# Gathers held twelve pairs back, a zone of 54 pairs, wider one-hots for lots, and waits by tile in one pool

## The chip, the cores and the metric

The kernel runs on one core of a Trainium2 chip. The metric is the device time of one execution in microseconds; a run's time is given beside the span that the profiler saw between the first and the last instruction.

## The reference

Three layers of a graph network with relations, on 6250 nodes of 256 features and 100000 edges, each with one of three types and 32 attributes; the edges come sorted by their target, and the targets crowd at low numbers (a squared uniform draw). Cut to what matters:

```python
ew = edge_attr @ edge_w + edge_b
rel_masks = [(edge_type == i).astype(x.dtype) for i in range(3)]
inv_cnt = [1.0 / jnp.maximum(segment_sum(m, dst, n), 1.0) for m in rel_masks]
x0 = x
for l in range(3):
    residual = x
    msg = relu(x[src] * ew)
    out = zeros((n, 256))
    for i in range(3):
        h = segment_sum(msg * rel_masks[i][:, None], dst, n) * inv_cnt[i][:, None]
        out = out + h @ weights[l, i]
    out = out + x @ roots[l] + biases[l]
    x = residual + relu(out)
return layernorm(x0 + x)
```

## The kernel before, in words

**Tiles and steps.** The edges are cut into tiles of 128, two tiles make a pair (391 pairs), two pairs a quad. For a quad the kernel fetches the source rows with indirect DMAs (one for each tile, so two a pair; `gather_pair`, L1458, issued by POOL into the ring of tiles `xs`, which has room for 8 quads), multiplies them with the edge weights (`weigh`, L873 on DVE), takes the relu (L874 on ACT), builds one-hots of the targets (`one_hot`), and sums the rows by target and relation with matmuls of rows and one-hots (`reduce`). A span is a run of pairs whose sums share a place in PSUM. Where the one-hot is the stationary operand (L911, L914) the sums come out turned: ACT copies them (`take`, L930), PE turns them back (`turn`, L934 and L936). `add` (L962, for lots L944) adds the sums to `acc`, which holds three relations of a window of nodes. When a block of 128 nodes is complete, matmuls with the layer's weights and root make its new rows (L975 to L1025).

**Zone and lots.** The first Z pairs are the zone: the low targets, where many edges share few nodes. Layers 1 and 2 don't go through them pair by pair. In layer 0 each zone quad's weights are kept (`keep_ew`, L800) and scattered row by row into a table in DRAM (`scatter`, L757 on POOL), in an order that a sort on DVE makes in groups of three tiles (L598 to L615). A class is one block of 128 source nodes with one relation (147 classes), and has room for 128 rows. In layers 1 and 2 the zone's edges come from that table by lots: a lot is a quad of up to four classes of one relation, a tile for each (39 lots a layer, 36 of them with four tiles). As a lot's tile has its sources in one block of x_all, PE picks their rows out of it (L836), and lots need no gather. Z came from `zone_of`, which takes the largest even number of pairs whose targets stay within 3 x 40 = 120 nodes: 52. The one-hot has 120 columns: WIN = 40 nodes by three relations for a common pair, 120 nodes of one relation for a lot.

**Order.** One loop over steps `it` (a step is a pair; 391 in layer 0, 391 - 52 + 75 = 414 in layers 1 and 2, of which 75 are lots' pairs) issues for each step, by hand: the sums of the pair of this step, the gathers of the pair AHEAD = 10 steps on, take, turn and add of spans that are done, weights and weighing and one-hots of the pair two steps on, and what a finished node block needs. In layer 0 the zone's quads are put in among the others, 7.1 steps apart, from step K + 114 on (K = 76), and the pairs from Z to 57 come as one block at K + 12. In layer 0, `keep_ew` also stores the weights of each quad beyond the zone to DRAM (L806 on ACT, L807 on SP), and `one_hot` its one-hots (L893, L895); layers 1 and 2 load both (L821 and L886 take them from the loaded tiles). So L890 makes one-hots from the targets in layer 0 and for lots alone.

**The wait of a gather.** `hold` adds to a gather a dependency on the sums of an earlier gathered pair: LEAD = 10 gathered pairs back (for the first 20 gathered pairs LEAD + HEAD = 12 back). `hold_early` does the same for the next layer's first 8 pairs. On POOL's queue a held gather holds what stands behind it: the next gathers and, in layer 0, the scatters that `after` puts behind each.

```python
        def hold(got, u, i):
            g = nth[u]
            if g >= LEAD + HEAD:
                behind(got, fetched[g - (LEAD if g >= 2 * LEAD else LEAD + HEAD)], i)
```

**Memory.** The pool `big` (L486) holds x_all, acc and inv. What lay at its place before is a pool of small tiles used at the start for looking at the indices (seg_o is made from its tiles by L1628). Without `reuse_waits="tile"` every tile of a pool waits until all readers of what the pool's place held are done; with it a tile waits for those alone whose memory it takes.

Of the kernel before, what the change touches and what calls it, by code (L numbers as in the profile page):

```python
# [442 lines left out]
def ordered_path(ctx, tc, x, attr_laid, A, weights, roots, biases, edge_w, edge_b, out, src, src_i, seg, place_i, consts, x_root,  # L443
# [41 lines left out]

    big = ctx.enter_context(tc.tile_pool(name="big", bufs=1))  # L486
    only = ExitStack()
# [205 lines left out]
    def layer(l, r_sb, b_sb, ats, early, ready, pools):  # L693
# [188 lines left out]
        def one_hot(q):  # L882
            ohs[q] = edge.tile([P, 4, WK], F32, name="oh", bufs=3)
            n = tiles_of(q)
            if q in oh_ls:
                nc.scalar.activation(ohs[q][:, :n], oh_ls[q][:, :n], AF.Copy)  # L886
                return
            for i in reversed(range(n)):
                at = zone[q][:, i // 2, i % 2, D:D + 1] if q in zone else seg[:, 4 * q + i:4 * q + i + 1]
                nc.vector.tensor_scalar(ohs[q][:, i, :], iota_w[:, :, :WIN], at, None, op0=ALU.is_equal)  # L890
            if l == 0:
                oh_bs[q] = early_pool.tile([P, 4, WK], BF, name="oh_b", bufs=3)
                nc.scalar.activation(oh_bs[q][:, :n], ohs[q][:, :n], AF.Copy)  # L893
                if 2 * q >= Z:
                    nc.sync.dma_start(oh_all[q][:, :n * WK], oh_bs[q][:, :n].rearrange("p t w -> p (t w)"))  # L895

        def reduce(u):
            span = span_of[u]
            bank, part = banks[span]
            first = opens(u) and part == 0  # L900
# [6 lines left out]
            if turned(span, last):  # L907
                for i in range(n):
                    t = u % 2 * 2 + i
                    if l == 0 and u // 2 in wide:  # L910
                        summed[u, i] = nc.tensor.matmul(h_p[:WK, :D + 1], ohs[u // 2][:, t, :], wide[u // 2][:, u % 2, i, :],  # L911
                                         start=(i == 0 and first), stop=(i == n - 1 and closes(u)), skip_group_check=True)
                        continue
                    summed[u, i] = nc.tensor.matmul(h_p[:WK, :D], ohs[u // 2][:, t, :], rows_of(u, i),  # L914
                                     start=(i == 0 and first), stop=(i == n - 1 and closes(u)), skip_group_check=True)
                    if l == 0:
                        summed[u, i] = nc.tensor.matmul(h_p[:WK, D:D + 1], oh_bs[u // 2][:, t, :], full_ones[:, 0:1],
                                         start=False, stop=(i == n - 1 and closes(u)), skip_group_check=True)
                return
            for i in range(n):  # L920
                for d in range(CH):
                    summed[u, i] = nc.tensor.matmul(h_p[:, d * WK:(d + 1) * WK],  # L922
                                     rows_of(u, i)[:, d * P:(d + 1) * P] if d < DC else full_ones,
                                     (ohs if d < DC else oh_bs)[u // 2][:, u % 2 * 2 + i, :],
                                     start=(i == 0 and d == 0 and first), stop=(i == n - 1 and closes(u)), skip_group_check=True)

        def take(span):
            n = D + 1 if l == 0 else D
            h_ss[span] = edge.tile([P, D + 1], F32, name="h_s", bufs=4)
            nc.scalar.activation(h_ss[span][:WK, :n], h_ps[span][:WK, :n], AF.Copy)  # L930

        def turn(span):
            for d in range(DC):
                nc.tensor.transpose(h_ps[span][:, d * WK:(d + 1) * WK], h_ss[span][:WK, d * P:(d + 1) * P], ident[:WK, :WK])  # L934
            if l == 0:
                nc.tensor.matmul(h_ps[span][:, DC * WK:(DC + 1) * WK], h_ss[span][:WK, D:D + 1].to_broadcast([WK, P]),  # L936
                                 ident[:WK, :WK], start=True, stop=True)

        def add(span):
            u = span[0]  # L940
            if u >= ZU:
                r = lots[u // 2 - ZU // 2][0]
                there = acc[:, :DC, r, ASIDE:ASIDE + WK]
                nc.vector.tensor_tensor(there, h_ps[span][:, :DC * WK].rearrange("p (c w) -> p c w", c=DC), there, op=ALU.add)  # L944
                return
# [271 lines left out]
EARLY = 8  # L1217
LEAD = 10
HEAD = 2
# [27 lines left out]
def zone_of(N, E):  # L1247
# [4 lines left out]
    v = 2  # L1252
    while v < U and node(2 * P * (v + 2)) * (1 + 6 / (2 * P * (v + 2)) ** 0.5) + 2 <= 3 * WIN:
        v += 2
# [213 lines left out]
def kernel(ctx, tc, x, src, dst, edge_attr, edge_type, weights, roots, biases, edge_w,  # L1468
# [11 lines left out]
    U = T // 2  # L1480
    WK = 3 * WIN
    K = schedule(N, E, 1, 0)[0][0]
# [7 lines left out]
    for name, width, value, kind in (("zero_o", 1, 0.0, F32), ("eps", 1, EPS, F32), ("full_ones", P, 1.0, BF)):  # L1490
        filled.append(keep.tile([P, width], kind, name=name))
        nc.vector.memset(filled[-1], value)
    iota_w = keep.tile([P, WK // WIN, WIN + GAP], F32, name="iota_w")
    nc.gpsimd.iota(iota_w, pattern=[[WIN, WK // WIN], [1, WIN + GAP]], base=0, channel_multiplier=0,
                   allow_small_or_imprecise_dtypes=True)
# [13 lines left out]
    with tc.tile_pool(name="look", bufs=1) as look, tc.tile_pool(name="look_p", bufs=2, space=PSUM) as look_p, \  # L1509
# [81 lines left out]
        tail = look.tile([P, 1], F32, name="tail")  # L1591
        for u, v, nodes in ((0, Z, WK), (Z, K, 2 * P)):
            nc.vector.tensor_reduce(tail, dst_t[:, 2 * u:2 * v], AX.X, ALU.max)
# [93 lines left out]
```

## Time and profile before

| | us |
|---|---|
| median of three runs | 3497.67 |
| lowest and highest run | 3482.07, 3502.85 |
| the profiled execution | 3495.29 |
| span of the profiled execution | 3493.3 |
| layer 0 / 1 / 2, stretches of the span | 1336 / 1062 / 1067 |
| PE, POOL busy | 2595.5 (74%), 2137.0 (61%) |
| DVE, ACT busy | 1897.1 (54%), 1891.7 (54%) |

In a profile "busy" is time in which an engine executes an instruction; PE is TensorE's matmuls and PEld its weight loads, DVE is VectorE, ACT ScalarE, POOL GpSimd, SP SyncE. "Idle before" an instruction is put down to what ended it last: `<-PE h_p L922` is an instruction of that line on that engine, "issue" is time for which the profile shows no wait, and "remote" a semaphore from an unknown source. An indirect DMA's busy time on POOL is the making of its descriptors, not the transfer.

### The profile page before, as it was taken

What the parts mean: (1) busy time and instruction counts of PE and PEld (TensorE: products, weight loads), DVE (VectorE), ACT (ScalarE), POOL (GpSimd) and SP (SyncE); (2) the same over time, 40 slices, a digit from 0 to 9 for tenths busy, and PEclk for the clock granted to TensorE, in tenths of its full rate; (3) what the DMA queues carried; (4) which work ended last, traced back from release to release, by engine and by line L of the source; (5) the groups of instructions that cost most, each with busy time, mean ns of one, the idle gap of its engine ahead of it and who ended that gap; (6) DMA issues with size and microseconds to landing.
All of it is one profiled execution on the core that took longest, in us unless ns stands there. A gap on an engine that the chain in (4) does not pass through costs nothing. (4 is left out here: it accounts for less than half of the span.)

```text
span 3493.3 us, 45265 instructions
## 1 busy us (share of the span) xinstructions
PE 2595.5 (74%) x12880; PEld 1999.6 (57%) x12880; DVE 1897.1 (54%) x4221; ACT 1891.7 (54%) x2580; POOL 2137.0 (61%) x2254
## 2 busy tenths in 40 slices
PE   5778777777777687777777777776777877778766
PEld 2445455555555455555566667665566666667665
DVE  6656555656555464444445555543445555566655
ACT  5666655555555555555554455554555655555555
POOL 6666666666666665666655566665666655565664
PEclk9889888888889899898988898888898999898888
DMA  7888555555555566767666676665776767766764
GB/s 247 274 261 257 189 179 182 177 174 174 173 172 173 165 194 220 229 215 223 211 202 205 203 224 216 216 212 160 257 235 219 230 220 223 227 215 222 225 216 153
DMA packets 358718, 730.97 MB, mean 209 GB/s; under 512 B 59082, under 2 KB 215804, under 8 KB 358332
## 3 DMA queue, kind: packets, MB, share of 16 engines
q1 hardware_dynamic: 243840, 426.68, 36.1%
q0 software_dynamic: 107616, 294.11, 28.4%
q10 hardware_dynamic: 7004, 7.19, 0.7%
q8 instruction: 107, 1.75, 0.2%
q14 instruction: 151, 1.24, 0.1%
HBM read 570.29 MB, written 157.46 MB: 208 GB/s over the span
## 5 line engine op out<-in xcount | busy, mean ns | idle before, releaser
L1458 POOL DMA_INDIRECT xs<-x_mid,src_r x1324 | 1255.9, 949 | 819.8 <-issue 396.8
L1458 POOL DMA_INDIRECT xs<-in_x_dram,src_io x770 | 734.3, 954 | 455.5 <-issue 161.8
L874 ACT ACTIVATE xs<-xs 128x1024 f32<-128x1024 f32 x533 | 560.4, 1051 | 767.1 <-DVE xs L873 484.5
L922 PE MATMUL h_p<-oh,xs 128*128 128x120 f32 x4608 | 716.1, 306 | 227.9 <-DVE acc L962 79.8
L922 PEld LDWEIGHTS h_p<-oh,xs 128*128 128x128 f32 x4608 | 671.7, 216 | 300.8 <-issue 115.7
L873 DVE TENSOR_TENSOR xs<-ew_p,xs 128x1024 f32<-128x1024 f32 x533 | 643.6, 1211 | 109.3 <-issue 48.9
L962 DVE TENSOR_TENSOR acc<-h_p,acc 128x240 f32 (+1 forms) x761 | 339.9, 449 | 662.7 <-remote 201.5
L991 PE MATMUL o_p<-w_sb,acc 128*128 128x256 f32 (+1 forms) x1752 | 505.3, 431 | 108.9 <-DVE acc L962 35.3
L991 PEld LDWEIGHTS o_p<-w_sb,acc 128*128 128x128 f32 (+1 forms) x1752 | 360.4, 216 | 209.9 <-issue 64.6
L914 PE MATMUL h_p<-xs,oh 128*120 128x256 f32 x1176 | 324.6, 409 | 80.9 <-ACT oh L886 24.9
L1022 DVE SCALAR_TENSOR_TENSOR x_root<-o_p,inv,x_root 128x256 f32<-128x256 f32 (+1 forms) x438 | 211.1, 482 | 303.4 <-PE o_p L991 93.3
L821 ACT ACTIVATE ew_p<-ew_s 128x1024 f32<-128x1024 f32 (+1 forms) x340 | 343.7, 1011 | 5.9 <-DMA ew_s<-ew_all 5.0
L914 PEld LDWEIGHTS h_p<-xs,oh 128*120 128x120 f32 x1176 | 222.6, 198 | 135.5 <-issue 50.4
L806 ACT ACTIVATE keep<-ew_p 128x1024 f32<-128x1024 f32 x170 | 172.4, 1014 | 202.0 <-remote 80.6
L850 PE MATMUL ew_p<-x_root,at 64*128 64x512 f32 x606 | 199.6, 738 | 79.1 <-issue 39.0
L911 PE MATMUL h_p<-xs,oh 128*120 128x257 f32 x772 | 213.4, 406 | 59.9 <-issue 36.6
L874 ACT ACTIVATE zone<-zone 128x1024 f32<-128x1024 f32 (+1 forms) x78 | 78.7, 1009 | 323.5 <-issue 156.6
L914 PE MATMUL h_p<-zone,oh 128*120 128x256 f32 x576 | 178.0, 447 | 99.8 <-ACT zone L874 36.8
L1008 ACT ACTIVATE acc<-zero_o 128x768 f32<-128x768 f32 (+1 forms) x150 | 141.4, 943 | 139.3 <-PE o_p L991 48.7
L836 PE MATMUL ew_p<-x_all,hot 128*128 128x256 f32 x588 | 164.5, 428 | 66.7 <-DVE hot L829 34.3
L890 DVE TENSOR_SCALAR oh<-iota_w,seg_o 128x120 f32<-128x120 f32 x782 | 207.8, 328 | 0.0
L911 PEld LDWEIGHTS h_p<-xs,oh 128*120 128x120 f32 x772 | 138.0, 191 | 109.3 <-issue 59.8
(182 smaller groups left out, 2870.3 us busy)
## 6 DMA issues: line engine op xcount, KB each, us to landing
ew_s<-ew_all SPq DMA_DIRECT2D x338, 512.0 KB
ew_all<-keep SPq DMA_DIRECT2D x169, 512.0 KB
oh_l<-oh_all SPq DMA_DIRECT2D x338, 120.0 KB
zone<-zone_table SPq DMA_DIRECT2D x72, 516.0 KB
xs<-x_mid,src_r POOLq DMA_INDIRECT x1324
oh_all<-oh_b SPq DMA_DIRECT2D x169, 120.0 KB
zone_table<-blank SPq DMA_DIRECT2D x21, 677.2 KB
x_mid<-x_all SPq DMA_DIRECT2D x98, 128.0 KB
```

What stands on the lines that cost most here:

```text
L821: nc.scalar.activation(ew_ps[q][:, :n], ew_ss[q][:, :n], AF.Copy)
L850: nc.tensor.matmul(ew_ps[q][:, k].rearrange("p i d -> p (i d)"), at[half, :], ew_sb[half].rearrange("p i d -> p (i d)"), start=False, stop ...
L873: nc.vector.tensor_mul(there, ew_ps[q][:, pairs.start:pairs.stop, :n], there)
L874: nc.scalar.activation(there, there, AF.Relu)
L890: nc.vector.tensor_scalar(ohs[q][:, i, :], iota_w[:, :, :WIN], at, None, op0=ALU.is_equal)
L911: summed[u, i] = nc.tensor.matmul(h_p[:WK, :D + 1], ohs[u // 2][:, t, :], wide[u // 2][:, u % 2, i, :], start=(i == 0 and first), stop=(i ...
L914: summed[u, i] = nc.tensor.matmul(h_p[:WK, :D], ohs[u // 2][:, t, :], rows_of(u, i), start=(i == 0 and first), stop=(i == n - 1 and closes ...
L922: summed[u, i] = nc.tensor.matmul(h_p[:, d * WK:(d + 1) * WK], rows_of(u, i)[:, d * P:(d + 1) * P] if d < DC else full_ones, (ohs if d < D ...
L962: nc.vector.tensor_tensor(there, h_ps[span][:, :CH * WK].rearrange("p (c r w) -> p c r w", c=CH, r=R), there, op=ALU.add)
L991: nc.tensor.matmul(o_p[:n, j, :], acc[:, d, r, slot:slot + n], w_sb[:, r * DC + d, :], start=(d == 0), stop=(d == DC - 1))
L1022: nc.vector.scalar_tensor_tensor(root, o_p[:n, j, :], inv[:n, c, r:r + 1], root, op0=ALU.mult, op1=ALU.add)
L1458: got = nc.gpsimd.indirect_dma_start(out=xs[:, u % 2, i, :], out_offset=None, in_=x_rows[:, :], in_offset=bass.IndirectOffsetOnAxis(ap=src ...
```

## The change

- `LEAD` goes from 10 to 12: a gather waits for the sums of the pair gathered twelve before it (the first 24 gathered pairs: fourteen before it). The steps at which gathers are issued stay.
- `zone_of` allows 128 nodes for 120: Z goes from 52 to 54. Layers 1 and 2 have 412 steps for 414, with as many lots, whose rows are fuller; pairs 52 and 53 are gathered in layer 0 alone, as a 27th quad of the zone (at step 374), whose weights go to the table, and no longer in the block at K + 12.
- A lot's one-hots, sums, takes, turns and adds are 128 columns wide (`wide_of`). The tile `oh` has room for 4 x 128; other pairs use 120 columns of each 128. L890 writes 128 columns in four pieces of 32 from an `iota_w` of four pieces, 40 apart, where it wrote 120 in one run from three pieces of 40, 48 apart.
- `big` gets `reuse_waits="tile"`.
- The look at the indices that decides whether this path can be used allows 128 nodes in the zone.

```diff
-    big = ctx.enter_context(tc.tile_pool(name="big", bufs=1))
+    big = ctx.enter_context(tc.tile_pool(name="big", bufs=1, reuse_waits="tile"))
...
         def one_hot(q):
-            ohs[q] = edge.tile([P, 4, WK], F32, name="oh", bufs=3)
+            hots_of = edge.tile([P, 4, P], F32, name="oh", bufs=3)
             n = tiles_of(q)
+            ohs[q] = hots_of if q in zone else hots_of[:, :, :WK]
...
-                nc.vector.tensor_scalar(ohs[q][:, i, :], iota_w[:, :, :WIN], at, None, op0=ALU.is_equal)
+                nc.vector.tensor_scalar(hots_of[:, i, :].rearrange("p (a b) -> p a b", a=4), iota_w[:, :, :P // 4], at, None,
+                                        op0=ALU.is_equal)
...
+        def wide_of(span):
+            return P if span[0] >= ZU else WK
+
...
-                    summed[u, i] = nc.tensor.matmul(h_p[:WK, :D], ohs[u // 2][:, t, :], rows_of(u, i),
+                    summed[u, i] = nc.tensor.matmul(h_p[:w, :D], ohs[u // 2][:, t, :], rows_of(u, i),
...
-                there = acc[:, :DC, r, ASIDE:ASIDE + WK]
-                nc.vector.tensor_tensor(there, h_ps[span][:, :DC * WK].rearrange("p (c w) -> p c w", c=DC), there, op=ALU.add)
+                there = acc[:, :DC, r, ASIDE:ASIDE + P]
+                nc.vector.tensor_tensor(there, h_ps[span][:, :DC * P].rearrange("p (c w) -> p c w", c=DC), there, op=ALU.add)
...
-LEAD = 10
+LEAD = 12
...
-    while v < U and node(2 * P * (v + 2)) * (1 + 6 / (2 * P * (v + 2)) ** 0.5) + 2 <= 3 * WIN:
+    while v < U and node(2 * P * (v + 2)) * (1 + 6 / (2 * P * (v + 2)) ** 0.5) + 2 <= P:
...
-    iota_w = keep.tile([P, WK // WIN, WIN + GAP], F32, name="iota_w")
-    nc.gpsimd.iota(iota_w, pattern=[[WIN, WK // WIN], [1, WIN + GAP]], base=0, channel_multiplier=0,
+    iota_w = keep.tile([P, 4, P // 4 + GAP], F32, name="iota_w")
+    nc.gpsimd.iota(iota_w, pattern=[[P // 4, 4], [1, P // 4 + GAP]], base=0, channel_multiplier=0,
...
-        for u, v, nodes in ((0, Z, WK), (Z, K, 2 * P)):
+        for u, v, nodes in ((0, Z, P), (Z, K, 2 * P)):
```

## Rows read from the trace of the kernel before

**Rows 1.** The page's span, and its part 1: busy us, share, instructions of each engine.

```profile
span 3493.3 us, 45265 instructions
PE 2595.5 (74%) x12880; PEld 1999.6 (57%) x12880; DVE 1897.1 (54%) x4221; ACT 1891.7 (54%) x2580; POOL 2137.0 (61%) x2254
```

**Rows 2.** By layer: stretch, us, PE/PEld/DVE/ACT/POOL busy (count), clock, DMA share, GB/s.

```profile
28.00:1364.00 1336.00, 1011.07 (x4896) 678.05 (x4897) 779.71 (x2007) 776.15 (x977) 842.91 (x884) 0.87 0.62 200
1364.00:2426.00 1062.00, 783.70 (x3978) 659.27 (x3976) 517.32 (x946) 536.66 (x750) 639.42 (x675) 0.87 0.68 213
2426.00:3493.00 1067.00, 792.74 (x3995) 660.35 (x3993) 579.25 (x1193) 573.83 (x852) 636.17 (x670) 0.88 0.68 217
```

**Rows 3.** The waits, whole span: engine, tile, line, what ended the wait; us, times, longest.

```profile
POOL xs L1458 <- issue: 564.1, 1485, 5.9
POOL xs L1458 <- PE h_p L922: 167.9, 157, 4.5
```

**Rows 4.** Groups by line, page's part 5: count, busy us, mean ns, idle before, releaser.

```profile
L1458 POOL DMA_INDIRECT xs<-x_mid,src_r x1324 | 1255.9, 949 | 819.8 <-issue 396.8
L1458 POOL DMA_INDIRECT xs<-in_x_dram,src_io x770 | 734.3, 954 | 455.5 <-issue 161.8
```

**Rows 5.** The view of line L873 on DVE: its idle time until a transfer (us, times).

```profile
  DMA xs<-in_x_dram,src_io: 5.7, 5
```

**Rows 6.** Timeline of the start: start, us, engine, line, operation, count, idle before.

```profile
21.62 1.28 ACT L498 ACT_TABLE_LOAD   x1 [21.62 <-DVE seg_o L1628]
22.92 2.12 ACT L498 ACTIVATE acc<-zero_o 128x2304 f32<-128x2304 f32 x1
25.98 1.23 DVE L873 TENSOR_TENSOR x_root<-ew_p,x_root 128x1024 f32<-128x1024 f32 x1 [4.12 <-ACT keep L806]
```

**Rows 7.** Groups by line, whole span.

```profile
L890 DVE TENSOR_SCALAR oh<-iota_w,seg_o 128x120 f32<-128x120 f32 x782 | 207.8, 328 | 0.0
L890 DVE TENSOR_SCALAR oh<-iota_w,zone 128x120 f32<-128x120 f32 x294 | 78.5, 328 | 0.0
L600 DVE TENSOR_SCALAR sort_hot<-iota_c,class_f 128x147 bf16<-128x147 bf16 x104 | 28.7, 276 | 0.0
L615 DVE TENSOR_REDUCE rank<-sort_hot 128x3 bf16<-128x441 bf16 (+1 forms) x35 | 21.4, 611 | 1.2
L821 ACT ACTIVATE ew_p<-ew_s 128x1024 f32<-128x1024 f32 (+1 forms) x340 | 343.7, 1011 | 5.9 <-DMA ew_s<-ew_all 5.0 <-issue 0.9
```

**Rows 8.** The view of line L671: ns min/median/max, first and last start.

```profile
L671 DVE TENSOR_SCALAR came<-came,next_i x16: 274/278/375, 922.3 to 1031.0; 128x128 f32<-128x128 int32 x16
```

**Rows 9.** Timeline of DVE around one-hots in layer 0, a first and a last lot.

```profile
27.13 1.06 DVE L890 TENSOR_SCALAR oh<-iota_w,seg_o 128x120 f32<-128x120 f32 x4
32.48 0.26 DVE L580 TENSOR_SCALAR before<-iota_c,node_i 128x128 bf16<-128x128 bf16 x1 [2.45 <-POOL iota_c L572]
...
1355.88 2.04 DVE L890 TENSOR_SCALAR oh<-iota_w,seg_o 128x120 f32<-128x120 f32 x8
1362.16 0.53 DVE L962 TENSOR_TENSOR acc<-h_p,acc 128x360 f32 x1 [4.24 <-issue]
...
1408.49 1.06 DVE L890 TENSOR_SCALAR oh<-iota_w,zone 128x120 f32<-128x120 f32 x4
1409.47 2.37 DVE L873 TENSOR_TENSOR xs<-ew_p,xs 128x1024 f32<-128x1024 f32 x2
...
3329.83 0.33 DVE L890 TENSOR_SCALAR oh<-iota_w,zone 128x120 f32<-128x120 f32 x1
3330.08 0.40 DVE L962 TENSOR_TENSOR acc<-h_p,acc 128x240 f32 x1
```

**Rows 10.** Timeline of DVE and of POOL about 69 us.

```profile
69.22 1.35 DVE L1002 TENSOR_TENSOR acc<-acc 128x1152 f32<-128x1152 f32 x1
69.30 2.08 POOL L1458 DMA_INDIRECT xs<-in_x_dram,src_io  x1 [0.30 <-issue]
```

More of the change, by code (lines that the diff above doesn't have):

```diff
@@ L895, in one_hot @@
                     nc.sync.dma_start(oh_all[q][:, :n * WK], oh_bs[q][:, :n].rearrange("p t w -> p (t w)"))
+        def wide_of(span):
+            return P if span[0] >= ZU else WK
         def reduce(u):
             span = span_of[u]
+            w = wide_of(span)
             bank, part = banks[span]
@@ L910, in reduce @@
                     if l == 0 and u // 2 in wide:
-                        summed[u, i] = nc.tensor.matmul(h_p[:WK, :D + 1], ohs[u // 2][:, t, :], wide[u // 2][:, u % 2, i, :],
+                        summed[u, i] = nc.tensor.matmul(h_p[:w, :D + 1], ohs[u // 2][:, t, :], wide[u // 2][:, u % 2, i, :],
                                          start=(i == 0 and first), stop=(i == n - 1 and closes(u)), skip_group_check=True)
                         continue
-                    summed[u, i] = nc.tensor.matmul(h_p[:WK, :D], ohs[u // 2][:, t, :], rows_of(u, i),
+                    summed[u, i] = nc.tensor.matmul(h_p[:w, :D], ohs[u // 2][:, t, :], rows_of(u, i),
                                      start=(i == 0 and first), stop=(i == n - 1 and closes(u)), skip_group_check=True)
                     if l == 0:
-                        summed[u, i] = nc.tensor.matmul(h_p[:WK, D:D + 1], oh_bs[u // 2][:, t, :], full_ones[:, 0:1],
+                        summed[u, i] = nc.tensor.matmul(h_p[:w, D:D + 1], oh_bs[u // 2][:, t, :], full_ones[:, 0:1],
                                          start=False, stop=(i == n - 1 and closes(u)), skip_group_check=True)
@@ L921, in reduce @@
                 for d in range(CH):
-                    summed[u, i] = nc.tensor.matmul(h_p[:, d * WK:(d + 1) * WK],
+                    summed[u, i] = nc.tensor.matmul(h_p[:, d * w:(d + 1) * w],
                                      rows_of(u, i)[:, d * P:(d + 1) * P] if d < DC else full_ones,
@@ L928, in take @@
             n = D + 1 if l == 0 else D
+            w = wide_of(span)
             h_ss[span] = edge.tile([P, D + 1], F32, name="h_s", bufs=4)
-            nc.scalar.activation(h_ss[span][:WK, :n], h_ps[span][:WK, :n], AF.Copy)
+            nc.scalar.activation(h_ss[span][:w, :n], h_ps[span][:w, :n], AF.Copy)
         def turn(span):
+            w = wide_of(span)
             for d in range(DC):
-                nc.tensor.transpose(h_ps[span][:, d * WK:(d + 1) * WK], h_ss[span][:WK, d * P:(d + 1) * P], ident[:WK, :WK])
+                nc.tensor.transpose(h_ps[span][:, d * w:(d + 1) * w], h_ss[span][:w, d * P:(d + 1) * P], ident[:w, :w])
             if l == 0:
@@ L1480 @@
     U = T // 2
-    WK = 3 * WIN
+    assert 3 * WIN <= P
     K = schedule(N, E, 1, 0)[0][0]
```

## The prediction, made before the changed kernel was run

> **What bounds the kernel now.** I read the page's head first: no engine fills the span. PE is busy for 2595.5 of 3493.3 us, POOL for 2137.0, DVE and ACT for 54% each [rows 1]. So the kernel is a loop of steps that the engines hand to each other, and what counts is the length of a step. The view by stretches gives it: layer 0 takes 1336 us for 391 steps, 3.42 us each; layer 1 takes 1062 us and layer 2 takes 1067 us for 414 steps, 2.565 and 2.577 us each [rows 2]. In layer 0, PE is busy for 1011 us (76%), DVE for 780 us (58%).
>
> Then the waits, since the change is named after the gathers. POOL stands before L1458 for long: 564.1 us are put down to issue, and 167.9 to the sums of L922 alone [rows 3]. By the groups it is 819.8 + 455.5 = 1275 us before 1324 + 770 = 2094 gathers [rows 4]. Of this the fixed issue time of 0.30 us that stands before a gather even when nothing holds it ("0.30 <-issue" [rows 10]) is 2094 x 0.30 = 628 us; the other 647 us is POOL being held back. The reader is to ask whether anyone behind POOL lacks those 647 us. The consumer of a gather is L873 on DVE. Its line shows idle time until a transfer into xs of 5.7 us, five times, in the whole span [rows 5]. So gathers are held because they are early: they wait for room, and the weighing hardly ever waits for them.
>
> **The change part by part.**
>
> *Gathers two pairs further ahead.* No instruction is added. Each gather's semaphore wait goes from the sums ten gathered pairs back to those twelve back, so POOL runs some two steps (5 to 7 us) earlier. Behind a held gather on POOL's queue stand the next gathers and, in layer 0, the scatters of the zone; these come earlier too. What waits for the landing is 5.7 us in all [rows 5], so the gain lies between 0 and 6 us if the idle times are named rightly. I take 0. The ends kept for the range are the rivals A and C.
>
> *Zone of 54 pairs for 52.* The lots keep their number (39 a layer) and get fuller; layers 1 and 2 lose two gathered pairs, 414 steps becoming 412. Two steps at the mean of their layer are 2 x (2.565 + 2.577) = 10.3 us [rows 2]. The lower bound is 0 (the two steps lie beside other waits), the upper 13, if they fall where steps are longer than the mean. I take 10.3. In layer 0 the steps stay 391: pairs 52 and 53 move to the end of the zone's row of quads. Their quad stores nothing for later layers (two SP stores fewer), but issues four scatters on POOL, each no dearer than a gather's 0.95 + 0.30 us, so 5 us, in the 224 us or so that POOL is held or idle in layer 0 (1336 less 842.91 busy less 884 x 0.30) [rows 2]. The sort gets one group more, nine DVE instructions: L598, three times L600 and L601, L613, L615; with 0.276 for seven and 0.611 for two that is at most 3.2 us [rows 7]. DVE is idle for 42% of layer 0, so I take 2 us with the added span's turn and add; without that cover it is some 5.
>
> *One-hots.* L890 wrote 120 elements from three pieces of 40 that lie 48 apart, in 328 ns, 782 times from seg_o and 294 times in the zone and lots [rows 7]. Now it goes over 4 x 32 on both sides. No row has that form. The nearest row with the same operation on 128 x 128 is L671, median 278 ns [rows 8]; the other bound is eight elements more at the old rate, 328 x 128/120 = 350 ns. I take 278, since the new form differs from L671 only in its gaps, and L890's 328 ns for fewer elements shows that the old form pays for something that L671 doesn't. That saves 50 ns x 4 = 0.20 us a quad. The Trainium skill, "VectorE: DVE Perf Modes", section "What auto-detection actually checks", says that a one-source operation in SBUF takes two elements a cycle if the outermost dimensions of source and destination are both even or equal; three against one long run of 120 is neither, four against four is. By that rule the saving would be as I take it, and if the rule doesn't hold it would be the loss of 22 ns apiece.
>
> How much of it shows? In layer 0 a saving of 195 x 0.20 = 39 us is made where DVE idles soon after: the last block, 2.04 us at 1355.88, is followed by 4.24 us of idle time [rows 9], and so are 174 of 194 in some measure (first at 27.13, with 2.45 us before the instruction at 32.48, last this one). The other 20 give 20 x 0.20 = 4 us. In the lots of layers 1 and 2 the block stands between two weighings with no gap (1408.49, then L873 at 1409.47 [rows 9]); 62 of 78 lots are like that (first this one, last at 3329.83, with L962 at 3330.08), at most 62 x 0.20 = 12 us. DVE is busy for only half of these layers, so what it gains is partly waited away later: half, 6 us. Sum 10; bounds: a loss of 1076 x 0.022 = 24 us and a gain of 39 + 12 = 51 us.
>
> The sums, takes, turns and adds of lots are 128 wide for 120, and L886 writes four runs with gaps for one. At a fifteenth of 0.33 us on some four instructions a lot it is at most 7 us over 78 lots, beside idle engines; I take 1.
>
> *Waits by tile in the big pool.* Everything in that pool waited for the readers of what lay there before. ACT's first instruction stands until L1628 is done (21.62); then its table load of 1.28 us and the zeroing of acc, 2.12 us from 22.92 on, stand ahead of the first keep, L806, so that it starts near 25. The first weighing awaits it, idle for 4.12 us [rows 6]. With waits by tile acc needn't wait for seg_o's making; x_all, whose memory was the same, still does. The first keep comes up to 1.28 + 2.12 = 3.4 us earlier, and the chain behind it by that less what POOL's iotas then hold; bounds 0 and 3.4, I take 2.5.
>
> **The sum** is made on the profiled execution, 3495.29 us (span 3493.3 and 2.0 around it), which lies 2.4 us, or 0.07%, under the median of the runs, 3497.67. 0 - 10.3 + 2 - 10 + 1 - 2.5 = -19.8, so 3475.5 us; on the median's ground 3478. I say 3477. A change under 1% (35 us) is about what a measurement of this kernel can't tell from none.
>
> **The rivals.**
>
> A. *The held time does matter.* The 647 us show that POOL is held, and a wait's label can be wrong where the label is "issue". If only one twentieth of it set the pace, the gain is 32 us more (3445); a fifth gives 129 (3348). For it: 564.1 us under a name that is no releaser [rows 3]. Against it: the 5.7 us at the consumer [rows 5].
>
> B. *Slower: the new one-hots stop the gathers.* At 69.22 a DVE operation of 1.35 us, L1002, ran beside a gather, and that gather took 2.08 us for 0.95 [rows 10]: DVE operations can hold POOL's descriptor work for about their length. If the four one-hots of a quad (4 x 0.278 = 1.11 us) do the same, POOL in layer 0 is occupied for 842.91 + 884 x 0.30 + 195 x 1.11 = 1324 of 1336 us [rows 2]: it becomes the pace. That happens from about 1.2 us a quad on; where scatters crowd (the zone's stretch) sooner, and with a loss of 5% in layer 0, or 60 us less the 20 of my sum, it gives 3495 + 40 = 3535. The Trainium skill, "GPSIMD Engine Reference", states that GpSimd shares SBUF interfaces with VectorE, contended by operations in a two-port mode or with two SBUF inputs; L1002 has two inputs and agrees, and the new one-hots would be of the first kind. Against B: POOL has slack in hand, and the 16 operations of L671 show only whether DVE is quick, not what POOL pays.
>
> C. *Earlier gathers meet other transfers.* The DMA engines are busy for 0.62 to 0.68 of the time [rows 2]. ACT waited for ew_s for just 5.0 us in all [rows 7]; if gathers shifted by two steps delayed one load in ten of 340 by 0.5 us, 17 us come back plus what follows: 3495 to 3505.
>
> D. *The one-hots keep their time or none of it shows*: 3495.3 - 10.3 - 2.5 + 3 = 3485.5, with 22 ns of loss each on the exposed ones up to 3490.
>
> E. *All of the one-hots' time shows*: 3475.5 - 41 = 3435.
>
> **How the numbers follow.** My forecast has 0.58, with its own range 3463 to 3484 for two steps between 0 and 13 and one-hots between 4 and 25. A has 0.14, B 0.06, C 0.05, D 0.12, E 0.05. The range of 3445 to 3507 takes the forecast, D, C and the low end of A: 0.8. Faster by over 1% is under 3463: A, E and the edge of the forecast, 0.14 + 0.05 + 0.06 = 0.25. Slower by over 1% is above 3533: B's upper part and unknown mishaps of C, 0.06. Within 1%: 0.69.
>
> **What would show it.** POOL's idle time before L1458 stays, less the two pairs, but with its waits on sums smaller, and L873 still waits for xs for under 10 us. Layers 1 and 2 are 5 to 8 us shorter each, layer 0 within 6 us of 1336. L890 has 274 to 290 ns. The first keep starts near 22 us. If L890 shows 350 ns, D holds; if gathers beside L890 show well over 0.95 us and POOL's busy time in layer 0 passes 900 us, B. If a layer's step falls by more than 3% (0.1 us in layer 0), A was right and the label of the waits wrong.

## The result, and the profile after

The changed kernel takes 3516.28 us at the median (3511.01 to 3535.09, 8 runs), the kernel before in the same series 3495.84: a ratio of 1.0074 with a 95% interval of 1.0046 to 1.0101, so some 20 us slower where 20 us less were forecast. Later series gave 1.0051 (1.0022 to 1.0080), 1.0034 (1.0004 to 1.0064) and 1.0051 (1.0023 to 1.0079).

One thing has to be known to read the experiments: in two of the series every kernel took about 600 us less, with the kernel before at 2889 and 2885 us where the other series had it at 3494 to 3497. The kernels don't decide it: all kernels of a series show the same, and the kernel before took 2889 us in one series and 3497 in another on one and the same chip. What decides it stayed open. Each comparison below is made within its own series, or between series of one setting by their ratios to the kernel before. I call the two settings the long and the short one; the prediction was made on a trace of the long one.

The page's head of the changed kernel, to be read against [rows 1]:

```profile
span 3512.0 us, 45182 instructions
PE 2578.8 (73%) x12870; PEld 1988.5 (57%) x12870; DVE 1855.0 (53%) x4232; ACT 1880.5 (54%) x2575; POOL 2134.9 (61%) x2250
```

No engine has more to do than before (DVE 42 us less), so the time went into waiting. By layer, as in [rows 2]:

```profile
25.00:1391.00 1366.00, 1006.21 (x4906) 675.89 (x4906) 749.38 (x2017) 770.52 (x977) 852.76 (x891) 0.86 0.62 198
1391.00:2428.00 1037.00, 774.95 (x3958) 648.98 (x3959) 510.96 (x944) 533.72 (x746) 628.58 (x665) 0.89 0.68 215
2428.00:3512.00 1084.00, 789.59 (x3994) 661.77 (x3992) 573.69 (x1194) 570.91 (x849) 635.30 (x669) 0.87 0.67 213
```

Layer 0 takes 1366 us for 1336, and POOL is busy in it for 852.76 us for 842.91, with the four scatters and the earlier start in it; layers 1 and 2 together take 2121 for 2129. The same by one line: L879 weighs the odd last pair of each layer, and its first start is the end of layer 0, its last that of layer 2. Before, and after:

```profile
L879 DVE TENSOR_TENSOR xs<-ew_p,xs x6: 414/415/417, 1363.6 to 3479.3; 128x256 f32<-128x256 f32 x6
```

```profile
L879 DVE TENSOR_TENSOR xs<-ew_p,xs x6: 415/416/417, 1391.1 to 3497.1; 128x256 f32<-128x256 f32 x6
```

Layer 0 ends 27.5 us later, although its first weighing began 3.1 us sooner (22.85 for 25.98 in [rows 6]). From the end of layer 0 to that of layer 2 it is 2106.0 us for 2115.7, or 9.7 us less. One trace against one says little of 10 us, since a second trace of the kernel before (before_2) has 2128.8; but over all traces of the long setting the four with a zone of 52 pairs have 2119 us on average (2112 to 2129) and the ten with 54 have 2105 (2092 to 2119): the two steps are there. So the whole loss, some 30 us, lies in layer 0.

The waits on POOL, as in [rows 3]:

```profile
POOL xs L1466 <- issue: 590.8, 1528, 7.2
POOL xs L1466 <- remote: 159.0, 101, 3.7
POOL xs L1466 <- PE h_p L928: 137.7, 151, 4.2
POOL zone_table L757 <- ACT keep L800: 45.6, 23, 3.8
```

And the groups that answer [rows 4] and [rows 7], with the scatters:

```profile
L1466 POOL DMA_INDIRECT xs<-x_mid,src_r x1316 | 1247.8, 948 | 814.1 <-issue 409.5 <-PE h_p L920 130.1 <-PE h_p L928 70.4
L1466 POOL DMA_INDIRECT xs<-in_x_dram,src_io x770 | 735.8, 956 | 428.2 <-issue 174.2 <-remote 86.0 <-PE h_p L928 66.7
L891 DVE TENSOR_SCALAR oh<-iota_w,seg_o 128x128 f32<-128x128 f32 x782 | 175.0, 298 | 0.0
L891 DVE TENSOR_SCALAR oh<-iota_w,zone 128x128 f32<-128x128 f32 x294 | 66.0, 302 | 0.0
L757 POOL DMA_INDIRECT zone_table<-keep,slot_i x108 | 106.2, 983 | 72.8 <-ACT keep L800 45.6 <-issue 24.5 <-DMA zone_table<-keep,slot_i 2.7
```

POOL waits for the sums of L928 for 137.7 us where it waited for those of L922 for 167.9, but its idle time before gathers falls only from 1275 us to 814.1 + 428.2 = 1242. A gather takes as long as before (948 and 956 ns). Those that ran beside a new one-hot took 958 ns on average, those beside no DVE instruction 947, so the new one-hots, at a mean of 298 ns, hardly slow POOL down. What is new is the last line of the waits: POOL stands before the scatters for a keep, 45.6 us. The scatters' group before:

```profile
L757 POOL DMA_INDIRECT zone_table<-keep,slot_i x104 | 102.0, 981 | 31.7 <-issue 28.6 <-ACT keep L806 1.2 <-ACT oh_b L893 1.2
```

There 31.7 us were little more than 104 times the fixed 0.30 us; now it is 72.8. The times of the single instructions show it more sharply: before, the first scatter of a quad starts 4.9 us behind the end of its keep at the median, and 2.4 at the least; now it is 0.28 us in each of the 27 quads, and POOL has stood for over 0.5 us before 26 of these 27 scatters.

### The profile page after: what moved, and what is told of

Read it like the earlier page. It is cut to its first block, busy times and chain, and to the rows that moved or that the text cites. A ratio compares the mean times of both kernels' runs of the same rounds, so it can differ in the third digit from the quotient of the medians.

```text
span 3512.0 us, 45182 instructions
## 1 busy us (share of the span) xinstructions
PE 2578.8 (73%) x12870; PEld 1988.5 (57%) x12870; DVE 1855.0 (53%) x4232; ACT 1880.5 (54%) x2575; POOL 2134.9 (61%) x2250
## 4 chain that ended last, share of the span: by engine, by line
PE 46%; issue 19%; DVE 12%; another core or an unknown queue 9%; ACT 7%; DMA 3%; POOL 2%; DVEq 1%; SPq 0%; ACTq 0%; POOLq 0%
PE h_p L928 11%; PE o_p L999 9%; PE h_p L920 9%; PE ew_p L850 4%; DVE xs L873 3%; PE r_p L983 3%; PE h_p L917 3%; PE ew_p L836 3%; DMA xs<-x_mid,src_r 2%; DVE x_root L1030 2%; PE h_p L942 2%; DVE acc L970 2%; POOL xs L1466 2%; DVE oh L891 1%
## 5 line engine op out<-in xcount | busy, mean ns | idle before, releaser
L1466 POOL DMA_INDIRECT xs<-x_mid,src_r x1316 | 1247.8, 948 | 814.1 <-issue 409.5
L1466 POOL DMA_INDIRECT xs<-in_x_dram,src_io x770 | 735.8, 956 | 428.2 <-issue 174.2
L928 PE MATMUL h_p<-oh,xs 128*128 128x120 f32 x4608 | 711.2, 305 | 228.8 <-issue 85.8
L928 PEld LDWEIGHTS h_p<-oh,xs 128*128 128x128 f32 x4608 | 666.8, 214 | 301.5 <-issue 110.3
L873 DVE TENSOR_TENSOR xs<-ew_p,xs 128x1024 f32<-128x1024 f32 x531 | 641.8, 1211 | 122.4 <-ACT keep L806 64.7
L999 PE MATMUL o_p<-w_sb,acc 128*128 128x256 f32 (+1 forms) x1752 | 497.8, 426 | 101.4 <-DVE acc L970 43.6
L821 ACT ACTIVATE ew_p<-ew_s 128x1024 f32<-128x1024 f32 x338 | 341.8, 1011 | 5.2 <-DMA ew_s<-ew_all 5.1
L920 PEld LDWEIGHTS h_p<-xs,oh 128*120 128x120 f32 x1160 | 218.1, 198 | 126.4 <-issue 35.7
L806 ACT ACTIVATE keep<-ew_p 128x1024 f32<-128x1024 f32 (+1 forms) x169 | 170.8, 1011 | 189.7 <-issue 176.8
L920 PE MATMUL h_p<-zone,oh 128*128 128x256 f32 x576 | 181.1, 453 | 98.5 <-ACT zone L874 43.4
L917 PE MATMUL h_p<-xs,oh 128*120 128x257 f32 x772 | 211.5, 402 | 45.6 <-issue 15.8
L836 PE MATMUL ew_p<-x_all,hot 128*128 128x256 f32 x588 | 155.7, 410 | 66.3 <-DVE hot L829 45.6
L920 PEld LDWEIGHTS h_p<-zone,oh 128*128 128x128 f32 x576 | 125.5, 228 | 129.4 <-ACT zone L874 73.1
L887 ACT ACTIVATE oh<-oh_l 128x480 f32<-128x480 bf16 x338 | 198.7, 588 | 0.0
```

The costliest lines, as they stand in the source:

```text
L821: nc.scalar.activation(ew_ps[q][:, :n], ew_ss[q][:, :n], AF.Copy)
L836: nc.tensor.matmul(ew_ps[q][:, i // 2, i % 2, :], hot[q][:, i, :], x_all[:, b + i, :], start=(i % 2 == 0), stop=(i % 2 == 1 or i == n - 1) ...
L873: nc.vector.tensor_mul(there, ew_ps[q][:, pairs.start:pairs.stop, :n], there)
L917: summed[u, i] = nc.tensor.matmul(h_p[:w, :D + 1], ohs[u // 2][:, t, :], wide[u // 2][:, u % 2, i, :], start=(i == 0 and first), stop=(i = ...
L920: summed[u, i] = nc.tensor.matmul(h_p[:w, :D], ohs[u // 2][:, t, :], rows_of(u, i), start=(i == 0 and first), stop=(i == n - 1 and closes( ...
L928: summed[u, i] = nc.tensor.matmul(h_p[:, d * w:(d + 1) * w], rows_of(u, i)[:, d * P:(d + 1) * P] if d < DC else full_ones, (ohs if d < DC ...
```

## The experiments

**First series: the short setting.** Four kernels: the changed one with LEAD at 10 (a_lead10) or the zone's bound at 3 * WIN (a_zone52), and the kernel before with one part done: LEAD at 12 (b_lead12), or one-hots from four pieces of 30 (b_hots). The number of pairs after which a gather is held, LEAD, is called room here; each expectation says what its theories (Lead, Hots, Zone and so on) hold to be the cause.

```diff
-LEAD = 12
+LEAD = 10
```

> The changed kernel with the gathers' wait put back to ten gathered pairs; all else as changed. The changed kernel takes 3516 us, the one before 3496. Theory Lead (gathers that run two pairs further ahead cost the 20 us net, and some 30 with the two steps and the start that are gained): 3480 to 3492, below the kernel before. Theory Hots (the quicker one-hots of L891 hold other engines up in layer 0): stays at 3512 to 3520. Theory Zone (the 27th quad of the zone, its scatters and its place cost it): stays at 3512 to 3520.

```diff
-    ... + 2 <= P:
+    ... + 2 <= 3 * WIN:
```

> The changed kernel with a zone of 52 pairs again (lots stay 128 wide). Theory Zone: 3480 to 3495. Theories Lead and Hots: the two steps in layers 1 and 2 come back, about 10 us, less 2 in layer 0, so 3520 to 3526.

```diff
-    nc.vector.tensor_scalar(ohs[q][:, i, :], iota_w[:, :, :WIN], at, ...
+    nc.vector.tensor_scalar(ohs[q][:, i, :].rearrange("p (a b) -> p a b", a=4), iota_w[:, :, :WK // 4], at, ...
```

> The kernel before with its one-hots alone changed: 120 columns from four pieces of 30 for three of 40, so that L890 takes about 280 ns for 328. Theory Hots: 3510 to 3520. Theories Lead and Zone: 3486 to 3496, the prediction's 10 us or nothing.

```diff
-LEAD = 10
+LEAD = 12
```

> The kernel before with the gathers' wait alone changed, twelve gathered pairs back for ten. Theory Lead: 3515 to 3530. Theories Hots and Zone: 3490 to 3500, as the prediction has it (0 us).

All four came within 0.2% of the kernel before, which took 2888.72 us: a_lead10 0.9988 (0.9978 to 0.9998), a_zone52 0.9984 (0.9974 to 0.9994), b_hots 1.0007 (0.9997 to 1.0016), b_lead12 0.9994 (0.9983 to 1.0006). The expectations were written for the long setting, and nothing is decided. The trace shows what sets the pace there; layer 0 of b_lead12, then its gathers:

```profile
28.00:1148.00 1120.00, 944.05 (x4889) 639.75 (x4890) 779.91 (x2005) 770.39 (x976) 845.19 (x883) 0.93 0.73 238
```

```profile
L1458 POOL DMA_INDIRECT xs<-x_mid,src_r x1324 | 1259.8, 951 | 432.8 <-issue 193.0 <-PE h_p L914 57.3 <-PE h_p L922 53.8
L1458 POOL DMA_INDIRECT xs<-in_x_dram,src_io x770 | 737.1, 957 | 235.6 <-issue 115.4 <-PE h_p L911 29.4 <-PE h_p L922 27.2
```

POOL is occupied for 845.19 + 883 x 0.30 = 1110 of 1120 us, and its idle time before the 2094 gathers of the whole span, 668 us, is 0.32 us for each: it is hardly ever held. There POOL is the pace of layer 0.

**Second series, long setting**: the changed kernel again, the kernel before for its trace, and the changed kernel without `reuse_waits="tile"` on the big pool.

> The changed kernel itself, once more, beside the kernel before. The four experiments so far found the kernel before at 2889 us, where the first comparison had 3496. If the loss belongs to the change: 1.005 to 1.010 of the kernel before. If it belongs to what made the first comparison's executions 600 us longer (long waits behind PE, a lower granted clock): 0.99 to 1.00, by the sum of the prediction 20 us below the kernel before, 2869 where that takes 2889.

> The kernel before, for its profile beside that of the changed one in the same place. Either theory: 2889 us as in the experiments so far or 3496 as in the first comparison; what is wanted is which waits make the difference of 600 us (the first comparison's waits behind PE that end with no named releaser, or a slower engine).

> The changed kernel without waits by tile in the big pool. By the prediction the tile waits are worth 2.5 us, so this is 2 to 3 us above the changed kernel. If the earlier start costs more than it gives (the first keep came 3 us sooner but the third quad was weighed 10.7 us later than before in the first comparison): 3 to 8 us below the changed kernel.

The changed kernel had 1.0051, a_bigpool 1.0037 (1.0008 to 1.0066): the tile waits are not what costs, and what they bring can't be seen in the total. before_2 took 3498.92 us with the waits of [rows 3] (586.3 us under issue), so those belong to the setting.

**Third series, long setting: one part at a time.** The new kernel here, a_lead8, is the changed one with both numbers at eight:

```diff
-    AHEAD = 10
+    AHEAD = 8
...
-LEAD = 12
+LEAD = 8
```

> The changed kernel with the wait put back to ten gathered pairs, once more: the first time the whole comparison took 2889 us for the kernel before, where layer 0 was paced by POOL's gathers without a pause. Where the kernel before takes about 3495: theory Lead (there, PE's signals reach their waiters only after POOL pauses, and gathers with more room pause later) expects 3480 to 3492, with the pauses before POOL's second scatter gone (a quad's keep ends some 5 us before its first scatter, as in the kernel before, and not 0.3 us); theories Hots and Zone expect 3508 to 3518. Where it takes 2889: 2884, as before.

> The changed kernel with gathers issued eight steps ahead and held for eight gathered pairs. Where the kernel before takes about 3495, theory Lead expects it below the one with ten: 3455 to 3485; theory Landing (less room makes gathers land too late, since they stood 15 us ahead at the median and 5.8 at the least) expects 3500 to 3540. Where it takes 2889, POOL has no pause to give and both expect 2885 to 2910.

> The kernel before with the wait alone put to twelve, once more. Where the kernel before takes about 3495: theory Lead expects 3515 to 3530, nearly all of it lost in layer 0; theories Hots and Zone 3490 to 3500. Where it takes 2889: 2886.

> The kernel before with its one-hots alone in four pieces, once more. Where the kernel before takes about 3495: theory Hots expects 3510 to 3520; theories Lead and Zone 3485 to 3496. Where it takes 2889: 2889.

| kernel | ratio to the kernel before (95%) | us |
|---|---|---|
| before + LEAD 12 (b_lead12_2) | 1.0100 (1.0062 to 1.0139) | 3530.02 |
| before + new one-hots (b_hots_2) | 1.0005 (0.9979 to 1.0030) | 3498.95 |
| changed, LEAD 10 (a_lead10_2) | 0.9968 (0.9941 to 0.9995) | 3486.51 |
| changed, 8 steps ahead, LEAD 8 (a_lead8) | 0.9935 (0.9906 to 0.9963) | 3474.40 |

This settles which part costs. The longer room alone makes the kernel before 35 us slower (22 to 49); with the room put back to ten, the changed kernel gains 11 us (2 to 21) where it lost 12 to 26 in the other series. Theories Hots and Zone fall, and so does Landing at eight. By line L879 the first ends layer 0 late and the second doesn't (b_lead12_2, then a_lead10_2):

```profile
L879 DVE TENSOR_TENSOR xs<-ew_p,xs x6: 414/415/416, 1387.1 to 3506.7; 128x256 f32<-128x256 f32 x6
```

```profile
L879 DVE TENSOR_TENSOR xs<-ew_p,xs x6: 412/414/416, 1362.1 to 3471.5; 128x256 f32<-128x256 f32 x6
```

And the scatters of the two: with room of twelve and ten steps ahead POOL stands before them, with ten it doesn't.

```profile
L757 POOL DMA_INDIRECT zone_table<-keep,slot_i x104 | 102.0, 981 | 77.9 <-ACT keep L800 43.7 <-issue 23.6 <-ACT ew_p L824 8.2
```

```profile
L757 POOL DMA_INDIRECT zone_table<-keep,slot_i x108 | 106.3, 985 | 32.9 <-issue 29.6 <-ACT xs L874 0.9 <-ACT keep L806 0.9
```

The other traces of the long setting agree: layer 0 ends between 1387.0 and 1394.1 us in all seven with a room of twelve and ten steps ahead, and between 1354.2 and 1368.7 in all six with less room.

**How room costs: the start.** In the changed kernel's timeline, out of several engines:

```profile
22.85 1.22 DVE L873 TENSOR_TENSOR x_root<-ew_p,x_root 128x1024 f32<-128x1024 f32 x1 [1.19 <-issue]
...
33.30 1.16 DVE L873 TENSOR_TENSOR x_root<-ew_p,x_root 128x1024 f32<-128x1024 f32 x1
34.38 0.86 DVE L891 TENSOR_SCALAR oh<-iota_w,seg_o 128x128 f32<-128x128 f32 x4
...
38.43 1.06 ACT L874 ACTIVATE x_root<-x_root 128x1024 f32<-128x1024 f32 x1 [9.12 <-remote]
...
41.43 0.95 POOL L1466 DMA_INDIRECT xs<-in_x_dram,src_io  x1 [0.30 <-issue]
46.43 0.94 POOL L1466 DMA_INDIRECT xs<-in_x_dram,src_io  x1 [4.06 <-PE h_p L923]
...
43.39 1.18 PE L920 MATMUL h_p<-x_root,oh 128*120 128x256 f32 x2 [11.54 <-issue]
```

(The first row is the first weighing, which answers [rows 6].) The second weighing, at 33.30, and its one-hots, at 34.38, are done by 35.3, yet the relu of that weighing starts at 38.43. PE, which waits behind it, stands for 11.54 us and goes on at 43.39, 3.9 us behind the end of the relu. POOL issues gathers without a pause all that time, up to 42.37, and then waits for PE for 4.06 us. The same place in three experiments, POOL's first gather after its first pause and PE's first long halt (a_lead8, a_lead10_2, b_lead12_2):

```profile
34.16 0.94 POOL L1466 DMA_INDIRECT xs<-in_x_dram,src_io  x1 [2.98 <-PE h_p L923]
...
36.34 1.16 PE L920 MATMUL h_p<-x_root,oh 128*120 128x256 f32 x2 [2.75 <-ACT x_root L874]
```

```profile
40.85 0.95 POOL L1466 DMA_INDIRECT xs<-in_x_dram,src_io  x1 [3.34 <-remote]
...
40.62 1.18 PE L920 MATMUL h_p<-x_root,oh 128*120 128x256 f32 x2 [8.91 <-issue]
```

```profile
51.81 0.94 POOL L1458 DMA_INDIRECT xs<-in_x_dram,src_io  x1 [3.46 <-remote]
...
53.68 2.08 PE L850 MATMUL ew_p<-x_root 64*128 64x512 f32 x4 [13.20 <-ACT ew_p L824]
```

POOL's first run without a pause ended at 34.16 - 2.98 = 31.2, 37.5, 42.4 (the changed kernel) and 48.4 us, and PE's halt ended at 36.3, 40.6, 43.4 and 53.7. (b_lead12_2 has the changed kernel's room, without its earlier start.) In 13 of the 14 traces of the long setting PE's first halt of over 2.5 us after 30 us ends 0.8 to 7.1 us behind POOL's first run (up to its first pause of over 0.55 us); in a_lead8 it also begins behind it, and a_lead6 has none. In the short setting b_lead12 has no such halt, and POOL runs on past 700 us. lead14 (of the fifth series below) has one, which ends at 37.71 while POOL runs on to 102 us:

```profile
35.07 0.25 DVE L580 TENSOR_SCALAR before<-iota_c,node_i 128x128 bf16<-128x128 bf16 x1 [8.28 <-POOL iota_c L572]
37.71 1.21 PE L920 MATMUL h_p<-x_root,oh 128*120 128x256 f32 x2 [5.89 <-ACT x_root L874]
```

It has a plain cause: the second weighing stands behind an instruction that needs iota_c, and POOL makes that behind its gathers, two pairs later with twelve steps ahead than with ten.

Counted over the semaphore events of four traces of the long setting (before, before_2, after, after_2): of 781 places where three or more of PE's signals (updates of semaphores) come within 0.3 us after at least 1 us without any, POOL was at work in one; it had been idle for 1.4 us at the median. In the six traces of the short setting there is no such place. As POOL itself often waits for those signals, the count alone proves no direction. The start speaks for one, that the signals wait for POOL's pause, since there POOL's run was what the experiments changed; it isn't proof, as LEAD and AHEAD move other waits too.

**Fourth series, long setting: standing before the scatters, or room as such.** ahead12 issues gathers twelve steps ahead (AHEAD = 12), which puts the scatters two pairs later on POOL's queue (and, beside that, iota_c behind two more pairs and the loads of the edges' attributes two steps earlier); head0 has HEAD = 0; a_lead6 has both numbers at six.

> The changed kernel with its gathers issued twelve steps ahead for ten, so that on POOL's queue the scatters stand behind gathers of two pairs later, as with a wait of ten. Where the kernel before takes about 3495: theory Scatter (POOL stands before scatters whose keep isn't there, 77 us of idle time for 31, and that costs the loss after the start) expects that idle time back at 31 to 35 us and 3490 to 3500; theory Signals (PE's signals come only when POOL pauses, and with more room it pauses later) expects 3508 to 3525 whatever the scatters do.

> The changed kernel with HEAD at 0, so that the first 24 gathered pairs are held for twelve pairs and not for fourteen. POOL's first run without a pause has 20 instructions in the changed kernel (to 42.4 us), and PE stands still until 1 us behind it. Where the kernel before takes about 3495: theory Signals expects POOL's first run 4 instructions shorter (to 37 us), the first halt of PE 5 us shorter and the kernel 4 to 8 us below the changed one (3504 to 3510); theory Scatter expects it unchanged, 3510 to 3516.

> The changed kernel with gathers issued six steps ahead and held for six gathered pairs. Where the kernel before takes about 3495, a wait of eight gave 3474 and one of ten 3487. Theory Signals alone expects another 5 to 15 us less, 3460 to 3470; theory Landing (gathers that stand 15 us ahead at the median with a wait of ten stand about 4 us ahead with six, and the weighing waits) expects 3500 to 3600, with L873 idle for transfers into xs for over 100 us, for 6 before.

> The changed kernel in the same series as these. 1.004 to 1.010 of the kernel before where that takes about 3495 (theories Lead, Signals and Scatter alike); where it takes 2889, the sum of the parts timed there so far (all but one part each: 0.9988 and 0.9984) expects 0.997 to 0.999.

Against 1.0034 for the changed kernel, ahead12 had 0.9995 (0.9968 to 1.0023), 14 us less by the ratios, with intervals that overlap a little. Its trace agrees with theory Scatter; the end of layer 0 in after_3, then layer 0 and scatters of ahead12:

```profile
L879 DVE TENSOR_TENSOR xs<-ew_p,xs x6: 412/414/415, 1392.4 to 3494.0; 128x256 f32<-128x256 f32 x6
```

```profile
L879 DVE TENSOR_TENSOR xs<-ew_p,xs x6: 412/412/416, 1375.8 to 3486.4; 128x256 f32<-128x256 f32 x6
```

```profile
L757 POOL DMA_INDIRECT zone_table<-keep,slot_i x108 | 105.9, 980 | 32.9 <-issue 30.5 <-ACT oh_b L895 0.9 <-ACT xs L874 0.6
```

The standing is gone (32.9 us for 108) and layer 0 ends at 1375.8 for 1392.4 of after_3. By these traces about half of what room costs came by way of the scatters (17 of 30 us). It is won where the scatters are: from the 61st weighing on, near the first scatter, the rest of layer 0 takes 983 us in ahead12, 989 to 1002 in the seven traces whose scatters stand, and 967 to 977 in the four with a room of ten. The rest of the loss stays with ahead12: a_lead10_2, whose scatters don't stand either, ended layer 0 at 1362.1 and had 0.9968. Some 7 us of it have arisen by the 61st weighing, when the scatters have hardly begun: it starts at 385 to 388 us with a room of ten, at 390 to 398 with twelve, and at 392.5 in ahead12. head0 had 1.0055 (1.0026 to 1.0083), a miss for theory Signals: POOL's first run ended at 38.1 and PE's halt was 7.7 us for 11.8, but layer 0 ended at 1392.2 all the same. What is won at the start is waited away later, so the start isn't the loss, and that late signals make the rest of the loss isn't shown.

a_lead6 had 0.9946 (0.9920 to 0.9972), no better than a_lead8. Here theory Landing begins to be right; the idle time of its weighing, as in [rows 5]:

```profile
  DMA xs<-x_mid,src_r: 122.7, 59
  DMA xs<-in_x_dram,src_io: 78.0, 28
```

That is 201 us for 6, less harmful than expected (3478.12 us for 3500 to 3600). PE's halts of over 2.5 us shrank in exchange, to 473 us for 542 in a_lead8, which fits but doesn't show why.

**Fifth and sixth series.** lead14 (AHEAD 12, LEAD 14) and ahead12h (AHEAD 12, LEAD 12, HEAD 0) fell into the short setting, the changed kernel after them into the long one.

> The changed kernel with gathers issued twelve steps ahead and held for fourteen gathered pairs, so that the scatters stand to the gathers' wait as in the changed kernel (ten and twelve). Where the kernel before takes about 3495, theory Signals (more room costs by itself: POOL's runs without a pause get longer) expects 8 to 20 us above the changed kernel, 3520 to 3532, the first halt of PE some 5 us longer (to about 48 us); theory Scatter alone expects the changed kernel's time, 3508 to 3516.

> The changed kernel with gathers issued twelve steps ahead, held for twelve, and HEAD at 0 (a first run of 16 to 18 instructions for 20). Where the kernel before takes about 3495, the same with HEAD at 2 took 3497. Theory Signals expects 3489 to 3494, the first halt 4 us shorter; theory Scatter alone 3495 to 3499.

> The changed kernel as a whole. Where the kernel before takes about 2885 us (POOL's gathers run there without a pause, and PE's signals reach their waiters at once), the runs with one part undone had 0.9984 and 0.9988, the one with more room 0.9961: 0.995 to 0.998, 2871 to 2880 us. The prediction's sum in full would be 20 us, 0.993. Where it takes about 3495: 1.003 to 1.008 once more.

lead14 had 0.9961 (0.9946 to 0.9976) of 2885.06 us, ahead12h 0.9980 (0.9970 to 0.9990), after_4 1.0051 of 3497.14. In the short setting more room costs nothing and may gain a little (b_lead12 alone had 0.9994), and the weighing there does wait for landings (b_lead12):

```profile
  DMA xs<-x_mid,src_r: 141.4, 63
  DMA xs<-in_x_dram,src_io: 16.5, 9
```

Whether the changed kernel as a whole gains there was not measured; every kernel near it had 0.996 to 0.999.

## Why the prediction was wrong, point by point

- *Gathers two pairs further ahead, taken at 0.* This is the step that failed. By itself it costs 35 us (22 to 49, b_lead12_2). The argument was that nobody behind POOL lacks the 647 us, and for gathers that is so: the weighing waits no more for transfers than before. But the prediction looked only at who waits for POOL and not at what POOL waits for next. It says itself that behind a held gather stand the scatters, and that "these come earlier too"; it gave that no price. A scatter needs the keep of its quad. As long as the gathers were held for the sums ten back, the keep was long done when POOL came to it; two pairs sooner, POOL gets there first and stands, 72.8 us for 31.7. By ahead12 about half of the loss came this way; what the other half waits for isn't known.
- *The label issue.* Rival A took 564.1 us under a name that is no releaser as a possible sign that gathers matter. Most of it was none: they are 1485 waits [rows 3], and 1485 x 0.30 = 446 us are the fixed time that the prediction had set aside two sentences on. The other 119 us were a sign, of something else: in the long setting PE's signals arrive late, and a fifth of them are missing from the trace. The longest such wait was 5.9 us where the fixed time is 0.30 [rows 3]; a wait that long with no releaser should have been followed up before any wait was declared harmless. Rival A itself, a gain, was wrong in sign there.
- *Zone.* Right in the main: 9.7 us less in layers 1 and 2 by the two first traces, 14 by the means of all, for 10.3. (POOL's slack in layer 0 is 228 us by the terms given, not 224; nothing hangs on it.) The cost of 2 in layer 0 can't be told apart; zone, one-hots and tile waits together gave 11 us (2 to 21, a_lead10_2) for some 20 in the sum.
- *One-hots.* Their own time is right in the main: 298 ns on average and 281 at the median for 278. The Trainium skill, "VectorE: DVE Perf Modes", section "What auto-detection actually checks", agrees with the traces: the form that is even on both sides is quicker with 128 columns than the old one with 120, and with the same 120 columns too (b_hots_2: 275 ns at the median for 328). But 10 us were to show and b_hots_2 has +2 (-7 to 10): rival D, though a gain of up to 7 us isn't excluded. Its layer 0 ended at 1361.3 us for 1363.6 and 1354.2 in the two traces of the kernel before, so what DVE saves there is waited away. The trace of b_hots_2 has the saving itself, L890 for [rows 7]:

```profile
L890 DVE TENSOR_SCALAR oh<-iota_w,seg_o 128x120 f32<-128x120 f32 x782 | 171.1, 294 | 0.0
```

- *Rival B*, the loss that was named, has the right sign and the wrong mechanism: gathers kept their 0.95 us, and POOL's busy time in layer 0 is 853 us where B was to show over 900.
- *Tile waits.* The first weighing came 3.1 us sooner for 2.5, as forecast, and by the third quad that was gone (weighed at 47.26 us for 36.53): the same halt that head0 shortens without effect. Without them (a_bigpool) the total is the same.
- *Rival C*, a collision of transfers: ACT waited 5.1 us for ew_s, as before; it did not happen.

**The version that beats both.** In the long setting a_lead8 takes 3474.40 us, 23 less than the kernel before (0.9935) and more below the changed one. That eight is better than ten (0.9968) isn't shown: the intervals overlap, and layer 0 ended at 1367.8 us for 1362.1. It was not timed in the short setting, where less room may cost, since the weighing waits there for landings already.

**What stays open.** Why signals are late in the long setting, and by what chain POOL's standing at a scatter lengthens layer 0, when POOL's own lateness reaches nobody through the gathers. Nor is it shown what ahead12 keeps of the loss: late signals, or what AHEAD moves beside the scatters, iota_c above all (made at 34.87 us for 29.63 in after_3, the second weighing at 35.53 for 33.45). lead14, which was to tell, ran in the other setting.

## What to carry to other kernels

A hold on an engine's queue also places what stands behind it: before loosening one, list the next instruction of every kind on that queue and ask what it will now wait for. That a held engine is early for its consumers proves only that loosening gains nothing, not that it costs nothing. And a prediction from one trace holds for the setting of that trace: the same longer room cost 1% in one setting here and nothing in the other.

## What the runs showed of the hardware that was not expected

- The same kernel takes 2885 to 2889 us in some series and 3494 to 3497 in others. DVE's and ACT's busy times agree (1897.0 and 1882.3 us in b_lead12, which differs from the kernel before in the gathers' wait alone, for 1897.1 and 1891.7 before), PE's is 2401.1 for 2595.5, and the mean granted clock 0.943 for 0.876. PE's halts of over 2.5 us from 25 us on number 36 with 142 us for 124 with 537. PE's longer busy time and its longer halts, 194 and 395 us, are nearly all of the 606 us between the two spans.
- In the long setting, waits behind finished work of PE and, at the start, of DVE last for microseconds beyond its recorded end; at the start PE's halt ends 0.8 to 7.1 us after POOL's first run of gathers does. PE's signals come in batches, some 190 to 200 a trace, nearly always while POOL is idle. In the short setting there are no such batches, and POOL issues nearly without a pause in layer 0.
- Traces of the long setting have fewer records of signals than the instructions send: 2720 for 3391 of PE before, and about half for DVE and ACT. In the short setting nearly all are there (3386 for 3399 of PE in b_lead12). So in the long setting the name of what ended a wait is less sure.
